# Distances of two graphs side by side in TensorE's row places

## The chip, the core and the metric

The kernel runs on one core of one Trainium2 chip. The metric is the time of one execution on the device, in microseconds. A core has a matrix engine (TensorE, "PE" in the profile, its weight loads "PEld"), a vector engine (VectorE, "DVE"), a scalar engine (ScalarE, "ACT"), a general engine (GpSimd, "POOL") and a queue engine (SyncE, "SP") which here only issues transfers. TensorE writes its products into PSUM, of which the pools of a stage take eight banks; the tiles in SBUF have 128 rows (partitions). Everything is in 32-bit floats.

## What is computed

64 graphs of 256 nodes with 256 features go through two layers. Layer 0 multiplies the normalised adjacency with the normalised rows and then with a weight. Layer 1 has a 17-tap convolution along the nodes, a message step, and a gated update. Cut to what matters here:

```python
# layer 0, h = relu(layernorm(x))
x = x + relu(einsum('bnm,bmf->bnf', norm_adj, h) @ W.T + b)
# layer 1, h = relu(layernorm(x))
x_conv = relu(bn2(conv17(relu(bn1(conv1(h))))) + h)
s    = h @ w_se.T + b_se                      # three numbers per node
dist = |s_n|^2 + |s_m|^2 - 2 s_n . s_m        # 256 x 256 per graph
A    = exp(-dist)                             # times the mask, here adj
x_nmp = einsum('bnm,bmd->bnd', A, relu(h @ w_msg.T + b_msg))
x = x + gru(concat(x_conv, x_nmp), h)
```

The distance matrix is what the change is about. It is written as a product with five rows: three hold the coordinates s, one holds ones against minus half the squared length, one the reverse. exp(2 x product) is then exp(-dist).

## The kernel before

**Stage one** (the loop over n, `for n in range(B + 4)`) takes the graphs through layer 0 and the front of layer 1 in a software pipeline. In turn n, TensorE gets, in this order: `turn_h` of graph n-2 (transposes, tile ht), `aggregate` of n (ag), `turn_cols` of n-3 (st), `turn_adj` of n+1 (at), `pass_messages` of n-4 (nm), `messages` of n-2 (ms), `distance` of n-3 (di), `project` of n (o) and `conv1` of n-2 (c). Between them calls of `item` slip in one piece of the convolution: first filter products (fs, `filter_part`), then spectra (df, `spectrum`), then products with the transformed filter (y, `product`). How many pieces enter is set by `pace`: its first entry is added at every call, its second is the running sum, and a piece goes when the sum passes one. While the filter is made only two of the eight calls per turn count.

The order on each engine is the order in which the program writes the instructions: `Pinned` keeps it on TensorE, ScalarE, VectorE and GpSimd. `after(k, f)` puts f off to the (k+1)-th following `beat`, so that the reading of a product is written some products later. `beat(us)` also releases the waiting elementwise work of the inverse transform (`Paced`), a share of the given time per engine. The transfers on SP are placed by a scheduler, as early as their tiles are free, but are then issued strictly in that order.

**The distance of one graph.** `messages` leaves three extra columns per node. `columns` (VectorE) copies them into the constant tile `cols` four times, at columns 0, 32, 64 and 96, and adds the squared lengths. `turn_cols` transposes `cols` (128 nodes x 128 columns, two blocks of nodes). ScalarE copies rows 0 to 36 into L and rows 64 to 100 into R. `distance` makes two products, one for each half of the nodes, with five rows each, at rows 0 and 32, into two banks: two row places of TensorE. ScalarE then takes two exponentials (tile e), GpSimd multiplies with the transposed adjacency `adjT` (tile aT), and a turn later `pass_messages` uses aT with the messages (msg).

The PSUM pool `ps` of stage one has five banks in rotation: ht, ag, st, at, nm, di, o, fs, df and y all take theirs from it. ms and c have banks of their own, which ScalarE fills with the bias ahead of the products.

**Filter.** When the tap weights are transposed and written out (wtd), two tiles tp are loaded from them by ten transfers, `pace[:] = FILTER / 2, -5.0` is set, and 32 filter pieces follow. Each has four products of 17 rows and 512 columns at rows 0, 32, 64 and 96 into four banks. The rest of the tp loads is issued as the pieces go.

**Convolution.** Its filter parts wf (71 per group of 16 graphs, 256 KB each) are loaded into `WF` buffers, and each product's end releases the next load. The inverse transform ends with `residual_load`, which brings rows of h2 into `hr` buffers.

**Gate stages.** Four times: the outputs are transposed (`turn_outputs`, yt), the spectra and first three products of the next group follow, then 16 graphs of gates, each with up to six products: one between the gates, the rest in a burst. Before the first, four products named `first_` with a 128-row identity touch the four gate banks.

Of the kernel before, what the change touches and what calls it, by code (L numbers as in the profile page):

```python
# [11 lines left out]
FP = mybir.dt.float32  # L12
AF = mybir.ActivationFunctionType
# [172 lines left out]
def gnn_kernel(  # L186
# [11 lines left out]
    P = 128  # L198
# [48 lines left out]
    def after(beats, go):  # L247
        due.append([beats, go])
# [66 lines left out]


    PARTS = [(0, 0), (0, 1)] + [(u, k) for u in range(1, UNITS) for k in (2, 1, 0)]
    WF = 8

    def wf_load(n):  # L320
        if n < len(PARTS):
# [43 lines left out]
    def inverse_after(u):  # L365

        if u == 7:
            inverse_three()
            for n in NS[:4]:
                residual_load(n)  # L370
        if u >= 8 and u % 4 == 3:
            inverse_group(u // 4 - 2)
        if u == UNITS - 1:
            inverse_last()
# [52 lines left out]
    def residual_load(n):  # L427

        src = h2_d[cv.q].rearrange("(p i) d -> p i d", i=OUT)
        cv.hr[n] = hr = cv.stream.tile([P, 2, D], FP, tag="hr", name=f"hr_{cv.q}_{n}", bufs=4)  # L430
        nc.sync.dma_start(hr, src[:, n::16, :])

    def inverse_last():
# [79 lines left out]
        for i in range(4):  # L513
            outs = points(i)
            paced.do(1, lambda i=i: done.add(i))
            paced.barrier(4, lambda i=i: i in done)
            for z in outs:
                outputs(NS[k], z, hold[k % 2])
                if k + 4 < len(NS):
                    paced.do(4, lambda k=k: residual_load(NS[k + 4]))  # L520
                residual(k + 2)
                k += 1

# [21 lines left out]
    with ExitStack() as one:  # L545
# [15 lines left out]
        def bank(name):  # L561
            return ps.tile([P, 512], FP, tag="ps", name=name)
# [20 lines left out]

        cols = wts.tile([P, NB, P], FP, tag="cols", name="cols")
        nc.gpsimd.memset(cols, 0.0)
        for c0 in (3, 35, 68, 100):
            nc.gpsimd.memset(cols[:, :, c0 : c0 + 1], 1.0)

        prep_stack = ExitStack()
        prep = prep_stack.enter_context(tc.tile_pool(name="prep", bufs=1))
# [425 lines left out]
        def conv1(g):  # L1018
            t = to_rows(g, "c1", w1T)

            def keep():
                h1 = work.tile([P, NB, D], FP, tag="c1", name=f"c1o_{g}")
                act.activation(h1, t, AF.Relu)
                nc.sync.dma_start(h1_d[g].rearrange("p (c d) -> p c d", c=NB), h1)
            after(1, keep)
            if g + 1 < B:
                after(2, lambda: own_bank("c1", g + 1, b1B))

        def messages(g):

            s, t = st[g], to_rows(g, "ms", wmT)

            def columns():
                four = cols.rearrange("p b (k w) -> p b k w", w=32)
                vec.tensor_copy(
                    four[:, :, :, 0:3],
                    t[:, :, D : D + 3].unsqueeze(2).broadcast_to([P, NB, 4, 3]),
                )
                sq = small.tile([P, NB, 3], FP, tag="sq", name=f"sq_{g}")
                vec.scalar_tensor_tensor(  # L1040
                    sq, cols[:, :, 0:3], -0.5, cols[:, :, 0:3], ALU.mult, ALU.mult
                )
                twice = sq.unsqueeze(2).broadcast_to([P, NB, 2, 3])
                vec.tensor_reduce(four[:, :, 0:2, 4], twice, AX.X, ALU.add)
                vec.tensor_reduce(four[:, :, 2:4, 3], twice, AX.X, ALU.add)

            def keep():
                s["msg"] = work.tile([P, NB, D], FP, tag="ms", name=f"mso_{g}", bufs=3)
                act.activation(s["msg"], t[:, :, :D], AF.Relu)
            after(1, columns)  # L1050
            after(1, keep)
            if g + 1 < B:
                after(2, lambda: own_bank("ms", g + 1, bmB))

        def turn_cols(g):
            s = st[g]
            t = bank(f"st_{g}")
            for nb in range(NB):
                pe.transpose(t[:, nb * P : (nb + 1) * P], cols[:, nb, :], ident)

            def keep():
                for key, p0 in (("L", 0), ("R", 64)):
                    s[key] = work.tile([37, N], FP, tag=key, name=f"{key}_{g}", bufs=1)
                    act.copy(s[key], t[p0 : p0 + 37, :N])
            after(1, keep)

        def distance(g):
            s = st[g]
            ts = [bank(f"di_{g}_{mc}") for mc in range(NB)]
# [7 lines left out]
            def weigh():  # L1077
                s["e"] = work.tile([P, NB, N], FP, tag="e", name=f"e_{g}")
                for mc in range(NB):
                    act.activation(s["e"][:, mc, :], ts[mc][:, :N], AF.Exp, scale=2.0)  # L1080

            def mask():
                s["aT"] = work.tile([P, NB, N], FP, tag="aT", name=f"aT_{g}")
# [91 lines left out]

        FILTER, SPECTRA, PRODUCTS = 2, 5, 3
        filtering = []
        for n in range(B + 4):
            even, odd = n % G == 0, n % G == 1
            if filtering and not items:  # L1180
                filtering.clear()
# [62 lines left out]
            if n >= 2 and later:  # L1244
                for go in later.pop(0):
                    go()
                if not later:
                    while due:
                        beat(0.0)
                    prep_stack.close()  # L1250
                    spec_stack = ExitStack()
                    spec = spec_stack.enter_context(tc.tile_pool(name="spec", bufs=1))
                    tab = spec.tile([P, 3 * UNITS], FP, tag="tab", name="tab")
                    nc.sync.dma_start(tab, nc.inline_tensor(filter_table(), name="tab_c").ap())
                    tp = {k: filter_load(k) for k in range(2)}
# [250 lines left out]
    for q in range(1, GROUPS + 1):  # L1506
# [7 lines left out]
        todo = []  # L1514
        if q < GROUPS:
            conv_begin(q)
            for k in range(WF):
                wf_load(k)
            for g in range(NG):
                for cb in range(DC):  # L1520
                    spectrum(g, cb)
            for u in range(1, AHEAD):
                sums(u)
            todo = [lambda u=u: product(u) for u in range(UNITS)]
            for _ in range(LEAD):
                todo.pop(0)()
# [45 lines left out]
```

## Time and profile before

| | us |
|---|---|
| median of 3 runs | 2120.74 |
| lowest, highest | 2119.82, 2123.37 |
| the profiled execution | 2119.19 |
| its span on the core | 2116.7 |
| TensorE busy in the span | 2068.2 |
| VectorE, ScalarE, GpSimd busy | 1414.1, 1017.0, 1098.9 |
| stage one, start to the first yt | 889.0 |
| spent on di by TensorE (256 records) | 44.8 |

How to read the rows. A 32-bit product is two records of TensorE, so one graph's distance, two products, is a group of four. Durations overlap, because products are pipelined: the cost of a group is the distance from its start to the next group's start. A timeline row gives start, duration, engine, line, operation, what is written from what, the number of instructions, and in brackets the idle time before it with what ended it. All work goes through one recording helper, so nearly every row has line 102: rows are told apart by tiles. The granted clock is the share of full speed that TensorE was given.

### The profile page before, as it was taken

What the parts mean: (1) busy time and instruction counts of PE and PEld (TensorE: products, weight loads), DVE (VectorE), ACT (ScalarE), POOL (GpSimd) and SP (SyncE); (2) the same over time, 40 slices, a digit from 0 to 9 for tenths busy, and PEclk for the clock granted to TensorE, in tenths of its full rate; (3) what the DMA queues carried; (4) which work ended last, traced back from release to release, by engine and by line L of the source; (5) the groups of instructions that cost most, each with busy time, mean ns of one, the idle gap of its engine ahead of it and who ended that gap; (6) DMA issues with size and microseconds to landing.
All of it is one profiled execution on the core that took longest, in us unless ns stands there. A gap on an engine that the chain in (4) does not pass through costs nothing. (4 is left out here: it accounts for less than half of the span.)

```text
span 2116.7 us, 31285 instructions
## 1 busy us (share of the span) xinstructions
PE 2068.2 (98%) x9977; PEld 1737.2 (82%) x9977; DVE 1414.1 (67%) x3207; ACT 1017.0 (48%) x2203; POOL 1098.9 (52%) x1309
## 2 busy tenths in 40 slices
PE   8979999999999999999999999999999999999998
PEld 6866666888888887688888888888888888888887
DVE  6545656545578998615989923989933889974444
ACT  5856666665455676542334442234452234443333
POOL 4333323334675565327766626767635767744343
PEclk9989999999999999999999999999999999999999
DMA  8696777755766554456533356533345523423331
GB/s 300 227 236 216 223 224 235 260 178 177 241 209 205 190 181 156 168 176 207 169 105 120 119 167 202 184 94 121 120 145 180 188 85 110 125 82 93 90 100 60
DMA packets 292458, 352.86 MB, mean 167 GB/s; under 512 B 19491, under 2 KB 232118, under 8 KB 291638
## 3 DMA queue, kind: packets, MB, share of 16 engines
q1 hardware_dynamic: 291680, 346.26, 52.2%
q0 software_dynamic: 288, 4.46, 0.6%
q8 instruction: 80, 1.31, 0.3%
q14 instruction: 84, 0.69, 0.1%
q10 hardware_dynamic: 326, 0.14, 0.0%
HBM read 224.43 MB, written 126.35 MB: 166 GB/s over the span
## 5 line engine op out<-in xcount | busy, mean ns | idle before, releaser
L102 DVE TENSOR_TENSOR Xf<-y,k 128x256 f32<-128x256 f32 x184 | 69.0, 416 | 180.9 <-PE y L102 178.6
L102 DVE SCALAR_TENSOR_TENSOR Xf<-Xf 128x256 f32<-128x256 f32 (+1 forms) x248 | 184.0, 757 | 6.5 <-ACT Xf L102 5.4
L102 PE MATMUL ta<-T,S 128*128 128x256 f32 x768 | 186.6, 379 | 0.0
L102 PE MATMUL y<-wf,Xf 128*128 128x256 f32 x768 | 182.5, 380 | 1.7 <-DVE Xf L102 1.4
L102 POOL TENSOR_TENSOR aT<-e,adjT 128x512 f32<-128x512 f32 x64 | 82.3, 1286 | 189.3 <-ACT e L102 189.3
L102 POOL TENSOR_TENSOR rz<-u,p 128x256 f32<-128x256 f32 x64 | 47.7, 745 | 244.8 <-ACT u L102 244.8
L102 ACT ACTIVATE rz<-rz 128x512 f32<-128x512 f32 x128 | 80.3, 627 | 180.3 <-DVE rz L102 180.3
L102 PEld LDWEIGHTS y<-wf,Xf 128*128 128x128 f32 x768 | 144.4, 190 | 24.4 <-DVE Xf L102 2.6
L102 PEld LDWEIGHTS ta<-T,S 128*128 128x128 f32 x768 | 145.9, 190 | 19.8
L102 PE MATMUL n<-wiT,hx 128*128 128x256 f32 x512 | 152.3, 379 | 0.0
L102 DVE SCALAR_TENSOR_TENSOR h2l<-rz,h2l 128x256 f32<-128x256 f32 x128 | 102.8, 803 | 53.4 <-POOL h2l L102 53.4
L102 POOL TENSOR_TENSOR xs<-Xf 128x256 f32<-128x256 f32 x92 | 71.0, 777 | 126.0 <-ACT Xf L102 64.1
L102 POOL TENSOR_TENSOR rs<-ve,mhalf 128x2 f32<-128x2 f32 (+1 forms) x65 | 46.9, 722 | 169.7 <-DVE nm L102 165.4
L102 POOL TENSOR_TENSOR adjH<-adjT,eye 128x512 f32<-128x512 f32 x64 | 82.0, 1282 | 97.4 <-ACT adjT L102 97.1
L102 PE MATMUL n<-whT,hx 128*128 128x256 f32 x512 | 131.4, 379 | 0.0
L102 PE MATMUL n<-wiT,xcT 128*128 128x256 f32 x512 | 131.4, 379 | 0.0
L102 PE MATMUL o<-w0T,aggT 128*128 128x256 f32 x512 | 127.8, 392 | 3.1 <-ACT aggT L102 3.1
L102 PE MATMUL ag<-adjH,hs 128*128 128x256 f32 x512 | 123.5, 384 | 4.7 <-POOL adjH L102 3.3
L102 PE MATMUL nm<-aT,mso 128*128 128x256 f32 x512 | 123.2, 384 | 4.2 <-POOL aT L102 3.4
L102 PE MATMUL ms<-wmT,h2T 128*128 128x259 f32 x512 | 124.7, 385 | 2.7 <-DVE h2T L102 2.7
L102 PE MATMUL c<-w1T,h2T 128*128 128x256 f32 x512 | 125.8, 390 | 0.0
L102 DVE BATCH_NORM_STATS2 st<-x 128x6 f32<-128x256 f32 x256 | 103.4, 404 | 28.2 <-DMA x<-in_x_dram 28.2
(185 smaller groups left out, 5319.7 us busy)
## 6 DMA issues: line engine op xcount, KB each, us to landing
wf<-wfd SPq DMA_DIRECT2D x284, 256.0 KB
wfd<-fo SPq DMA_DIRECT2D x32, 576.0 KB
x2d<-x SPq DMA_DIRECT2D x64, 256.0 KB
h2d<-h SPq DMA_DIRECT2D x64, 256.0 KB
hTd<-h2T SPq DMA_DIRECT2D x64, 256.0 KB
h1d<-c1o SPq DMA_DIRECT2D x64, 256.0 KB
xnd<-xnT SPq DMA_DIRECT2D x64, 256.0 KB
h1l<-h1d SPq DMA_DIRECT2D x64, 256.0 KB
```

The source lines that it names most:

```text
L102: return self.tc.keep_in_program_order(getattr(self.engine, op)(*args, **kwargs))
```

## The change

- `cols` gets a second side and each graph of a pair its own columns. Sides L and R are separate 128-column halves; row place 32k holds half m of the nodes of graph b, with k = 2m + b. `columns` of a graph writes its own places, `turn_cols` and `distance` run in even turns only and serve two graphs. There are four transposes per pair, one copy each for L and R with all 128 rows, and four products at four row places into four banks.
- The exponentials of the second graph are put one beat behind those of the first, its mask two beats behind.
- `turn_cols` and `distance` are at n-4, `pass_messages` at n-5, the loop has one turn more; adjT gets a sixth buffer, msg a fourth. The last `conv1` moves from turn B+1 to B+2.
- The filter's pace starts at -7 in place of -5.
- WF is 6 in place of 8, the residual loads have 3 buffers in place of 4 and are asked for three outputs ahead. In the gate stages the first wf loads are written between the last spectra, no longer ahead of all.
- The `first_` products use 32 rows each, at four row places.

```diff
-    WF = 8
+    WF = 6
...
-            for n in NS[:4]:
+            for n in NS[:3]:
                 residual_load(n)
...
-        cv.hr[n] = hr = cv.stream.tile([P, 2, D], FP, tag="hr", name=f"hr_{cv.q}_{n}", bufs=4)
+        cv.hr[n] = hr = cv.stream.tile([P, 2, D], FP, tag="hr", name=f"hr_{cv.q}_{n}", bufs=3)
...
-                if k + 4 < len(NS):
-                    paced.do(4, lambda k=k: residual_load(NS[k + 4]))
+                if k + 3 < len(NS):
+                    paced.do(4, lambda k=k: residual_load(NS[k + 3]))
...
-        cols = wts.tile([P, NB, P], FP, tag="cols", name="cols")
+        cols = wts.tile([P, NB, 2, P], FP, tag="cols", name="cols")
         nc.gpsimd.memset(cols, 0.0)
-        for c0 in (3, 35, 68, 100):
-            nc.gpsimd.memset(cols[:, :, c0 : c0 + 1], 1.0)
+        for k in range(4):
+            nc.gpsimd.memset(cols[:, :, 0, 32 * k + 3 : 32 * k + 4], 1.0)
+            nc.gpsimd.memset(cols[:, :, 1, 32 * k + 4 : 32 * k + 5], 1.0)
...
-                s["adjT"] = work.tile([P, NB, N], FP, tag="adjT", name=f"adjT_{g}", bufs=5)
+                s["adjT"] = work.tile([P, NB, N], FP, tag="adjT", name=f"adjT_{g}", bufs=6)
...
-                four = cols.rearrange("p b (k w) -> p b k w", w=32)
+                own = cols.rearrange("p b s (m k w) -> p b (s m) k w", m=2, k=2)[:, :, :, g % 2]
                 vec.tensor_copy(
-                    four[:, :, :, 0:3],
+                    own[:, :, :, 0:3],
                     t[:, :, D : D + 3].unsqueeze(2).broadcast_to([P, NB, 4, 3]),
                 )
...
-                s["msg"] = work.tile([P, NB, D], FP, tag="ms", name=f"mso_{g}", bufs=3)
+                s["msg"] = work.tile([P, NB, D], FP, tag="ms", name=f"mso_{g}", bufs=4)
...
         def turn_cols(g):
             s = st[g]
-            t = bank(f"st_{g}")
-            for nb in range(NB):
-                pe.transpose(t[:, nb * P : (nb + 1) * P], cols[:, nb, :], ident)
+            t = bank(f"st_{g}").rearrange("p (s n) -> p s n", s=2)
+            for side in range(2):
+                for nb in range(NB):
+                    pe.transpose(
+                        t[:, side, nb * P : (nb + 1) * P],
+                        cols[:, nb, side, :], ident,
+                    )
 
             def keep():
-                for key, p0 in (("L", 0), ("R", 64)):
-                    s[key] = work.tile([37, N], FP, tag=key, name=f"{key}_{g}", bufs=1)
-                    act.copy(s[key], t[p0 : p0 + 37, :N])
+                for side, key in enumerate("LR"):
+                    s[key] = work.tile([P, N], FP, tag=key, name=f"{key}_{g}", bufs=1)
+                    act.copy(s[key], t[:, side])
             after(1, keep)
 
         def distance(g):
-            s = st[g]
-            ts = [bank(f"di_{g}_{mc}") for mc in range(NB)]
-            for mc in range(NB):
-                own_rows = slice(32 * mc, 32 * mc + 5)
+            both = [(b, mc) for mc in range(NB) for b in range(2)]
+            ts = [bank(f"di_{g + b}_{mc}") for b, mc in both]
+            for k, (b, mc) in enumerate(both):
+                own_rows = slice(32 * k, 32 * k + 5)
                 pe.matmul(
-                    ts[mc][:, :N], s["L"][own_rows, mc * P : (mc + 1) * P],
-                    s["R"][own_rows, :], start=True, stop=True,
+                    ts[k][:, :N], st[g]["L"][own_rows, mc * P : (mc + 1) * P],
+                    st[g]["R"][own_rows, :], start=True, stop=True,
                 )
...
-            after(1, weigh)
-            after(2, mask)
+            after(1, lambda: weigh(0))
+            after(2, lambda: weigh(1))
+            after(2, lambda: mask(0))
+            after(4, lambda: mask(1))
...
-        for n in range(B + 4):
+        for n in range(B + 5):
...
-            if 3 <= n <= B + 2:
-                turn_cols(n - 3)
+            if even and 4 <= n <= B + 2:
+                turn_cols(n - 4)
...
-            if n >= 4:
-                pass_messages(n - 4)
+            if n >= 5:
+                pass_messages(n - 5)
...
-            if 3 <= n <= B + 2:
-                distance(n - 3)
+            if even and 4 <= n <= B + 2:
+                distance(n - 4)
...
-            if 2 <= n <= B + 1:
+            if 2 <= n <= B:
                 conv1(n - 2)
+            elif n == B + 2:
+                conv1(B - 1)
...
-                    pace[:] = FILTER / 2, -5.0
+                    pace[:] = FILTER / 2, -7.0
...
-    for tag, bufs in (("ta", 1), ("tc", 1), ("n", 2)):
-        for k in range(bufs):
-            t = ps_gate.tile([P, 2 * D], FP, tag=tag, name=f"first_{tag}_{k}", bufs=bufs)
-            pe.matmul(t, ident, brzB, start=True, stop=True)
+    for r, tag in enumerate(("ta", "tc", "n", "n")):
+        t = ps_gate.tile([P, 2 * D], FP, tag=tag, name=f"first_{r}", bufs=1 + (tag == "n"))
+        at = slice(32 * r, 32 * (r + 1))
+        pe.matmul(t, ident[at, :], brzB[at, :], start=True, stop=True)
...
             conv_begin(q)
-            for k in range(WF):
-                wf_load(k)
             for g in range(NG):
+                if g >= NG - WF:
+                    wf_load(g - NG + WF)
                 for cb in range(DC):
                     spectrum(g, cb)
```

More of the change, by code (lines that the diff above doesn't have):

```diff
@@ L1033, in columns @@
             def columns():
-                four = cols.rearrange("p b (k w) -> p b k w", w=32)
+                own = cols.rearrange("p b s (m k w) -> p b (s m) k w", m=2, k=2)[:, :, :, g % 2]
                 vec.tensor_copy(
-                    four[:, :, :, 0:3],
+                    own[:, :, :, 0:3],
                     t[:, :, D : D + 3].unsqueeze(2).broadcast_to([P, NB, 4, 3]),
                 )
+                s3 = own[:, :, 0, 0:3]
                 sq = small.tile([P, NB, 3], FP, tag="sq", name=f"sq_{g}")
-                vec.scalar_tensor_tensor(
-                    sq, cols[:, :, 0:3], -0.5, cols[:, :, 0:3], ALU.mult, ALU.mult
-                )
+                vec.scalar_tensor_tensor(sq, s3, -0.5, s3, ALU.mult, ALU.mult)
                 twice = sq.unsqueeze(2).broadcast_to([P, NB, 2, 3])
-                vec.tensor_reduce(four[:, :, 0:2, 4], twice, AX.X, ALU.add)
-                vec.tensor_reduce(four[:, :, 2:4, 3], twice, AX.X, ALU.add)
+                vec.tensor_reduce(own[:, :, 0:2, 4], twice, AX.X, ALU.add)
+                vec.tensor_reduce(own[:, :, 2:4, 3], twice, AX.X, ALU.add)
             def keep():
-                s["msg"] = work.tile([P, NB, D], FP, tag="ms", name=f"mso_{g}", bufs=3)
+                s["msg"] = work.tile([P, NB, D], FP, tag="ms", name=f"mso_{g}", bufs=4)
                 act.activation(s["msg"], t[:, :, :D], AF.Relu)
@@ L1077, in weigh @@
-            def weigh():
-                s["e"] = work.tile([P, NB, N], FP, tag="e", name=f"e_{g}")
+                    ts[k][:, :N], st[g]["L"][own_rows, mc * P : (mc + 1) * P],
+                    st[g]["R"][own_rows, :], start=True, stop=True,
+                )
+            def weigh(b):
+                s = st[g + b]
+                s["e"] = work.tile([P, NB, N], FP, tag="e", name=f"e_{g + b}")
                 for mc in range(NB):
-                    act.activation(s["e"][:, mc, :], ts[mc][:, :N], AF.Exp, scale=2.0)
@@ L1082, in mask @@
-            def mask():
-                s["aT"] = work.tile([P, NB, N], FP, tag="aT", name=f"aT_{g}")
+                    act.activation(s["e"][:, mc, :], ts[2 * mc + b][:, :N], AF.Exp, scale=2.0)
+            def mask(b):
+                s = st[g + b]
+                s["aT"] = work.tile([P, NB, N], FP, tag="aT", name=f"aT_{g + b}")
                 pool.tensor_tensor(s["aT"], s["e"], s["adjT"], ALU.mult)
-            after(1, weigh)
-            after(2, mask)
+            after(1, lambda: weigh(0))
```

## The prediction

> **What bounds the kernel now.** I read the page's busy rows first, then where TensorE waits, then the stretches around those waits. TensorE is the bound nearly everywhere: busy for 2068.2 of 2116.7 us, and the work that this change touches is TensorE's own.
>
> ```profile
> PE 2068.2 (98%) x9977; PEld 1737.2 (82%) x9977; DVE 1414.1 (67%) x3207; ACT 1017.0 (48%) x2203; POOL 1098.9 (52%) x1309
> ```
>
> So first: what does one distance cost TensorE? The timeline of TensorE in a steady stretch of stage one (start, duration, group):
>
> ```profile
> 709.59 1.91 PE L102 MATMUL ms<-wmT,h2T 128*128 128x259 f32 x8
> 711.43 0.70 PE L102 MATMUL di<-R,L 5*128 5x256 f32 x4
> 712.06 1.99 PE L102 MATMUL o<-w0T,aggT 128*128 128x256 f32 x8
> 713.89 1.89 PE L102 MATMUL c<-w1T,h2T 128*128 128x256 f32 x8
> 715.62 0.60 PE L102 MATMUL ht<-ident,h 128*128 128x128 f32 x4
> ```
>
> Read starts, not durations. From di to o is 0.63. From ms to di is 1.84, and eight ms matmuls take 1.75 where no di follows: 0.09 more. From o to c is 1.83, against 1.73 from c to ht, also eight matmuls of 256 columns: 0.10 more. One distance costs 0.63 + 0.09 + 0.10 = 0.83 us, for two products side by side.
>
> Four row places side by side exist already, in the filter's products (fs). Same view, two of its groups:
>
> ```profile
> 165.66 1.68 PE L102 MATMUL fs<-tp,tab 17*72 17x512 f32 x8
> 167.27 2.02 PE L102 MATMUL ms<-wmT,h2T 128*128 128x259 f32 x8
> ...
> 171.77 1.09 PE L102 MATMUL fs<-tp,tab 17*72 17x512 f32 x8
> 172.79 1.99 PE L102 MATMUL c<-w1T,h2T 128*128 128x256 f32 x8
> ```
>
> With all banks free four products of 512 columns take 1.02 (171.77 to 172.79), about the length of one. At 165.66 the same group takes 1.61: its fourth bank was still held.
>
> Two places where TensorE is not the bound matter here. At 144 us it waits 11.47 us, and the chain of waits leads to a load (TensorE, ScalarE and VectorE timelines):
>
> ```profile
> 155.42 2.25 PE L102 MATMUL fs<-tp,tab 17*72 17x512 f32 x4 [11.47 <-ACT e L102]
> 157.60 3.58 PE L102 MATMUL c<-w1T,h2T 128*128 128x256 f32 x8
> ```
> ```profile
> 153.83 0.60 ACT L102 ACTIVATE mso<-ms 128x512 f32<-128x512 f32 x1 [13.73 <-DVE cols L102]
> ```
> ```profile
> 151.49 0.43 DVE L102 BATCH_NORM_STATS2 st<-x 128x6 f32<-128x256 f32 x1 [15.13 <-DMA x<-in_x_dram]
> ```
>
> VectorE is stuck on the row moments of x_14, ScalarE on VectorE, TensorE on both. The c after it takes 3.58 instead of 1.89: the granted clock averages 0.68 between 140 and 160 us. The second place is the end of stage one:
>
> ```profile
> 874.86 0.70 PE L102 MATMUL di<-R,L 5*128 5x256 f32 x4
> 878.59 3.78 PE L102 MATMUL nm<-aT,mso 128*128 128x256 f32 x8 [3.03 <-POOL aT L102]
> 883.09 2.08 PE L102 MATMUL first_ta<-brzB,ident 128*128 128x512 f32 x2 [0.72 <-ACT xnT L102]
> 884.95 1.91 PE L102 MATMUL first_tc<-brzB,ident 128*128 128x512 f32 x2
> 886.66 2.49 PE L102 MATMUL first_n<-brzB,ident 128*128 128x512 f32 x4
> 888.99 0.27 PE L102 MATMUL yt<-ident,Xf 128*128 128x128 f32 x1
> ```
>
> **The change, part by part.**
>
> *Distances.* 64 visits become 32. A visit's surroundings stay (0.09 + 0.10); its middle is 0.63 plus two more starts, 7 ns apart in the fs group: 0.65. So 32 x (2 x 0.83 - 0.84) = 26.1 us less. The transposes of cols are as many as before (two per graph, 0.11 each). The copies of L and R halve (64 x 0.36 of ScalarE less), and VectorE's four small operations per graph stay.
>
> *What the four banks may cost.* Stage one has five rotating banks; a pair now holds four. The Trainium skill (TensorEngine Tiling (Array Packing), Performance Considerations, PSUM Bottleneck) says that tiling speeds up TensorE but not the emptying of PSUM, which may become the bound. In the rows at 129 to 132 us the exponentials start 1.55 us after di starts (131.29 against 129.74, behind mso and a bias copy) and two take 0.65. Four end at 2.85, with some 0.2 to reach TensorE 3.05. By the rule TensorE would stand there from 2.46 (0.63 + o's 1.83) on: 0.6 x 32 = 19 us given back in place of the 4.4 below, and a time of 2104.5. By the rows it mostly does not: o takes the fifth bank, and behind it c1 has its own. Only the filter's second group follows o directly with rotating banks; there 8 to 9 pairs wait about 0.5, +4.4. Against it stands the filter's first group: in odd graphs no L and R copies precede adjT, so its fourth bank is free sooner, 8 x 0.6, and in even ones the doubled transposes give the copies 0.2 more, -1.6. I take -2; bounds -7 and +4.4.
>
> *Messages a graph later.* n + 5 in place of n + 4; the extra turn holds one product that was there before, so it is a shift. adjT and msg get a buffer each. The first mask ends some 3.5 us after di starts (1.29 of GpSimd behind the exponentials), its nm comes after o, c, ht, ag and at, at 6.8; the second is needed a graph later. I cost it at nothing; if that cover were gone, 1.3 per pair.
>
> *The stall at 144 us.* Filter -5 to -7 moves the first filter product by two slots, one graph. x_14 stays behind the ten tp loads on SP, and its moments stay ahead of cols_9 on VectorE, so the stall stays. Only how early it begins changes: TensorE has less to do ahead of it (nm_7, the first fs group, di_8 left for later: 1.73 + 1.5 + 0.43, some 3.9 with st). The release is the second half of hs_12 on ScalarE, about 4.3 us after x_14's first moments, and the load comes earlier by what TensorE gained until graph 7. That is at most 4.2 (0.83 x 5 - 0.84 x 2 + one nm), and about 2.8 where ScalarE, without idle time from 56 to 67 us, holds the pace. The next ag starts at 151.5 - 2.8 + 4.3 = 153.0; adding 3.9 of owed work and 2.8 for the halved clock, equal progress stands at 159.7 against 161.45: 1.75 gained where the distances counted so far (9 visits against 4.5 pairs) claim 3.7. So +2; bounds -2 and +4.
>
> *End of stage one.* Before, from ms_63's end (869.94) to yt (888.99): 19.05. After, from the same point: wait for cols_63 1.3, st 0.44, nm_61 1.73 (earlier work before), switch 0.1, di pair 0.64, switch 0.1, c1_63 1.73 (moved here), wait for aT_62 about 0.6, nm_62 and nm_63 3.46, xnT's bank 1.0, four first products side by side 1.15. Sum 12.25, less nm_61 10.5, so 8.5 shorter, of which 0.83 is already a distance: -7.7. The clock stays up[...]. VectorE's and GpSimd's inverse work is now issued later; its first outputs end at about +8, before yt at +12.25. If it is late: down to -4; if the waits vanish: -9.
>
> *Less time per graph under VectorE.* From 700 to 870 us VectorE is busy 147.4 of 170 us and TensorE already loses about 4 us in waits for h2T, hs and pre. TensorE's share per graph falls by 0.41, VectorE's does not. +2.5; bounds 0 and +6.
>
> *WF 8 to 6, residual buffers 4 to 3.* I matched the queue's packets in order with SP's issues: in the bursts of five products a wf lands 1.6 to 3.4 us after its issue, and with eight buffers the tightest has 3.0 us in hand. Two fewer take away 2 x 0.865: 1.27 left. Residual loads land 2.3 us after issue; moved one output later they still come 0.7 us ahead of GpSimd. In the changed program the gate stages' first six wf loads still stand on SP behind the last products, ahead of the stage. All at nothing; bounds -1 and +3.
>
> *Start.* The zeroing of cols is twice as wide and ahead of eye on GpSimd: +0.3.
>
> Sum: -26.1 - 2 + 2 - 7.7 + 2.5 + 0.3 = -31.0. The profiled execution took 2119.19 (span 2116.7), so 2088.2; the median of the runs, 2120.74, lies 1.55 above it: **2089.7 us**.
>
> **Rivals.**
>
> *Slower: TensorE waits once per pair for the second graph's exponentials or mask.* The second exponentials and mask are issued a beat and two beats behind the first. For it: ScalarE carries four at once, as in the rule above. Against it: 3.3 us lie between the first mask and its nm, a graph more for the second, and o has the fifth bank. It decides from 31.0/32 = 0.97 us per pair on; at 1.3, the whole second mask uncovered, the time is 2131. Chance 0.05.
>
> *Half the gain: VectorE or the banks give it back.* Both at their bad ends (+3.5, +6.4) and the end of stage one at -4: 2103; the rule's sum, 2104.5, belongs here. Chance 0.15.
>
> *More: the stall at 144 us goes.* If x_14 comes before TensorE needs VectorE, 11.5 of waiting and 3.7 of slow clock go, and the +2: about 2073. Against it: the ten tp loads keep their place ahead of x_14. Chance 0.07.
>
> *The four do not run side by side.* Then a visit takes 1.28 and only the switches are saved, 0.19 x 32 = 6: 2110. Against it: fs at 171.77. Chance 0.04.
>
> **How the numbers follow.** The likeliest case holds 0.69, its own range 2081 to 2099. Reaching into the half-gain case above and partly toward the vanished stall below gives 2079 to 2104. About 0.2%, 4 us, is what a measurement can tell from no change. Only the slow case ends above 2125, so slower 0.05; within, 0.02 from the edges of the second and fourth; faster 0.93.
>
> **What would show it.** Right: di in 32 groups of eight, 0.64 to 0.65 each; a stall of 10 us or more on x_14 still there, now at ag; yt 8 us nearer to ms_63; the granted clock near 1 at the end of stage one; wf never in TensorE's waits. Wrong: di groups split by bank waits, TensorE waiting for e or aT in most pairs, wf among its waits in the bursts of five products, or VectorE above nine tenths with waits of a microsecond per graph.

## The result and the profile after

| | us |
|---|---|
| before, median of the runs beside it | 2120.51 |
| after, median (lowest, highest) | 2087.19 (2086.44, 2090.9) |
| ratio after to before, 95% interval | 0.9844 (0.9827 to 0.9861) |
| the profiled execution after, its span | 2086.44, 2084.7 |

The forecast of 2089.7 was 2.5 us too high. That closeness is luck: four of its terms are off by 2 to 6 us each, and they cancel. Where the time went, stretch by stretch, in the two traces (idle is TensorE's idle time in the stretch, gaps of all sizes summed):

| stretch | before | after |
|---|---|---|
| start to the stall on x_14: idle | 10.8 | 12.5 |
| the stall | 11.5 | 10.2 |
| stall to 680 us: idle | 2.0 | 0.7 |
| 680 us to the last ms: idle | 4.2 | 8.9 |
| start of the last ms | 868.1 | 836.8 |
| last ms to the first yt (idle) | 20.8 (3.9) | 15.9 (4.2) |
| first yt to the first df behind it (idle) | 7.8 (0.0) | 11.6 (2.4) |
| from there to the end | 1219.9 | 1220.4 |

The page of the kernel after, TensorE's row:

```profile
PE 2029.4 (97%) x9977; PEld 1728.8 (83%) x9977; DVE 1413.3 (68%) x3207; ACT 987.4 (47%) x2139; POOL 1101.0 (53%) x1313
```

TensorE is busy 38.8 us less with the same number of records, and its idle time has grown: 97% in place of 98%. A steady pair of the kernel after, in TensorE's timeline (start, duration, group):

```profile
697.58 1.91 PE L102 MATMUL ms<-wmT,h2T 128*128 128x259 f32 x8
699.42 0.71 PE L102 MATMUL di<-R,L 5*128 5x256 f32 x8
700.07 1.99 PE L102 MATMUL o<-w0T,aggT 128*128 128x256 f32 x8
701.90 1.89 PE L102 MATMUL c<-w1T,h2T 128*128 128x256 f32 x8
703.62 0.60 PE L102 MATMUL ht<-ident,h 128*128 128x128 f32 x4
```

Four products take 0.65 from di to o where two took 0.63. Of the 32 visits 31 are groups of eight records, 0.644 in the median; the one at 604 us is cut into six and two by a wait of 0.27. The turn of an odd graph has no di, and there ms costs 1.75 and o 1.73, so the switches on both sides (0.09 and 0.10) are saved too. 32 x (2 x 0.826 - 0.839) = 26.0.

The filter's groups, same view (behind nm and behind o in an odd turn, then behind nm in an even one):

```profile
169.28 1.44 PE L102 MATMUL fs<-tp,tab 17*72 17x512 f32 x8
170.65 2.02 PE L102 MATMUL ms<-wmT,h2T 128*128 128x259 f32 x8
172.51 1.89 PE L102 MATMUL o<-w0T,aggT 128*128 128x256 f32 x8
174.32 1.09 PE L102 MATMUL fs<-tp,tab 17*72 17x512 f32 x8
...
207.95 1.22 PE L102 MATMUL fs<-tp,tab 17*72 17x512 f32 x8
209.10 1.58 PE L102 MATMUL ms<-wmT,h2T 128*128 128x259 f32 x6
```

From start to start they take, behind nm, 1.37 in odd and 1.15 in even turns (before 1.61 or 1.92), behind o 1.24 or 1.02. Leaving out the first one of each trace, 31 groups take 37.0 us after and 46.9 before. In the kernel before, two of them took 3.07, which the prediction had not looked for. One of the two, TensorE's timeline before:

```profile
297.32 1.08 PE L102 MATMUL fs<-tp,tab 17*72 17x512 f32 x4
299.38 1.08 PE L102 MATMUL fs<-tp,tab 17*72 17x512 f32 x4 [0.98 <-DVE pre L102]
300.39 3.43 PE L102 MATMUL c<-w1T,h2T 128*128 128x256 f32 x8
303.62 0.89 PE L102 MATMUL ht<-ident,h 128*128 128x128 f32 x4
```

Its third product waits for VectorE to finish reading o's bank, and here c and ht behind it run at half speed: 3.23 and 0.73 from start to start, where 1.83 and 0.44 are usual.

The stall on x_14 is still there, now at ag. VectorE's and TensorE's timelines after:

```profile
146.45 0.43 DVE L102 BATCH_NORM_STATS2 st<-x 128x6 f32<-128x256 f32 x1 [13.62 <-DMA x<-in_x_dram]
```
```profile
139.82 0.60 PE L102 MATMUL ag<-adjH,hs 128*128 128x256 f32 x2
150.60 2.93 PE L102 MATMUL ag<-adjH,hs 128*128 128x256 f32 x6 [10.18 <-ACT hs L102]
```

Between 680 us and the last ms TensorE waits for VectorE's copy h2T. The longest of these waits cost more than itself:

```profile
777.17 3.53 PE L102 MATMUL ms<-wmT,h2T 128*128 128x259 f32 x8 [2.07 <-DVE h2T L102]
780.49 2.11 PE L102 MATMUL o<-w0T,aggT 128*128 128x256 f32 x8
```

From start to start ms and o take 3.32 and 1.94 here, where 1.75 and 1.73 are usual: 1.8 of half-speed clock, which is no idle time and so is not in the table.

The end of stage one after, in the timelines of TensorE, of ScalarE and of SP's issues:

```profile
844.72 3.72 PE L102 MATMUL nm<-aT,mso 128*128 128x256 f32 x16 [0.28 <-POOL aT L102]
851.55 1.14 PE L102 MATMUL first<-brzB,ident 32*128 32x512 f32 x8 [3.12 <-ACT xnT L102]
852.63 0.48 PE L102 MATMUL yt<-ident,Xf 128*128 128x128 f32 x1
852.89 0.42 PE L102 MATMUL yt<-ident,scr 128*128 128x128 f32 x1
...
857.88 1.94 PE L102 MATMUL yt<-ident,Xf 128*128 128x128 f32 x14 [2.44 <-ACT xcT L102]
```
```profile
850.94 0.56 ACT L102 COPY xnT<-nm 128x512 f32<-128x512 f32 x1
...
857.14 1.26 ACT L102 ACTIVATE xcT<-yt,sh 128x512 f32<-128x512 f32 x2 [2.71 <-DMA xnd<-xnT]
```
```profile
853.04 0.53 SPq L431 DMA_DIRECT2D hr<-h2d  x1
853.68 0.54 SPq L1113 DMA_DIRECT2D xnd<-xnT  x1
```

The first yt comes 36.4 us earlier than before (852.6, was 889.0), but df only 32.6: yt now stops for 2.44 us. ScalarE may not write xcT until the last xnT has been stored, whose memory xcT takes over, and that store is issued on SP behind a residual load.

### The profile page after: what moved, and what is told of

Read it like the earlier page. It is cut to its first block, busy times and chain, and to the rows that moved or that the text cites. A ratio compares the mean times of both kernels' runs of the same rounds, so it can differ in the third digit from the quotient of the medians.

```text
span 2084.7 us, 31178 instructions
## 1 busy us (share of the span) xinstructions
PE 2029.4 (97%) x9977; PEld 1728.8 (83%) x9977; DVE 1413.3 (68%) x3207; ACT 987.4 (47%) x2139; POOL 1101.0 (53%) x1313
## 5 line engine op out<-in xcount | busy, mean ns | idle before, releaser
L102 POOL TENSOR_TENSOR rs<-ve,mhalf 128x2 f32<-128x2 f32 (+1 forms) x65 | 46.9, 722 | 231.5 <-DVE nm L102 226.6
L102 PE MATMUL ag<-adjH,hs 128*128 128x256 f32 x512 | 123.4, 384 | 15.9 <-ACT hs L102 10.8
L102 PEld LDWEIGHTS ms<-wmT,h2T 128*128 128x128 f32 x512 | 95.9, 191 | 34.9 <-issue 13.5
```

The lines of the kernel that those rows point to most:

```text
L102: return self.tc.keep_in_program_order(getattr(self.engine, op)(*args, **kwargs))
```

## The experiments

Times are medians, each with its ratio to the kernel before on the same chip; the kernel before had 2120.3 to 2122.2 there.

**1. Pairs split.** The second graph's two products in the odd turn, all else as changed.

```diff
...
-            if even and 4 <= n <= B + 2:
-                distance(n - 4)
+            if 4 <= n <= B + 3:
+                distance(n - 4 - n % 2, n % 2)
```

> The changed kernel (2087.2), but the second graph of a pair has its two distance products in the following, odd turn: 64 visits of two products again, at the same row places, with the transposes, the copies of L and R, the extra buffers, the end of stage one and the filter's start all left as changed. If each saved visit is worth what the prediction counted, 2 x 0.83 - 0.84 per pair comes back: +26.1, 2113. Rival from the trace after: the time per graph between 700 and 850 us is already set by VectorE there, so that 12 to 16 pairs lost half of their saving; then what comes back is 18 to 21, 2105 to 2108. Second reading: the filter's first groups take 1.26 on average where they took 1.7, and two long groups of 3.07 are gone; if that comes from the distance's banks being absent in odd turns, it comes back too, 7 to 11 us, and the first rival is hidden under it; if it comes from the halved copies and the filter's new place, the groups stay at 1.26.

Measured: 2105.8, ratio 0.9933 (0.9921 to 0.9945), so the split costs 18.6 us and not 26.1. TensorE's timeline with the pairs split, an odd turn and the last nm:

```profile
196.48 1.11 PE L102 MATMUL fs<-tp,tab 17*72 17x512 f32 x8
197.52 2.02 PE L102 MATMUL ms<-wmT,h2T 128*128 128x259 f32 x8
199.47 0.70 PE L102 MATMUL di<-R,L 5*128 5x256 f32 x4
200.10 1.99 PE L102 MATMUL o<-w0T,aggT 128*128 128x256 f32 x8
...
864.66 1.99 PE L102 MATMUL nm<-aT,mso 128*128 128x256 f32 x8 [3.02 <-POOL aT L102]
```

The visit costs the old 0.63 and the switches, 26.0 in all, so something comes back the other way. Pairs do cost banks: with them, 31 filter groups take 37.0 and not 35.5, and two di behind y wait 0.5 and 1.0. The stall is 1.2 shorter without pairs, and between 680 us and the last ms TensorE waits 5.0 in place of 8.9. Together 1.5 + 1.5 + 1.2 + 3.9 = 8.1, and half clock behind the stall and at 777 us takes 2.5 more from the pairs. Against that, the split kernel loses 4.8 between its last ms and df that are no distances: its last nm stands 3.02 for aT, yt 4.21. In the two traces 26.0 - 8.1 - 2.5 + 4.8 = 20.2, where the spans differ by 19.5. So the 18.6 hold a worse end of stage one, and the pairs by themselves bring less. The filter's groups behind nm stay short (1.04 and 1.46). So the shorter groups behind nm do not come from pairing.

**2. The filter's start back at -5.**

```diff
-                    pace[:] = FILTER / 2, -7.0
+                    pace[:] = FILTER / 2, -5.0
```

> The changed kernel with the filter's start back at -5. The prediction's step: the stall on x_14 stays either way, and -7 only moves work that is done ahead of it or after it, so within 2 us of 2087.2. Theory from the trace after: the inverse work of the first group now ends too late for the end of stage one (TensorE waits 3.1 us ahead of first and 2.4 us in yt, both behind ScalarE's and VectorE's inverse work); with the filter one graph earlier that work ends a graph earlier and 3 to 5 us go: 2082 to 2084. Rival: the filter's place in the turns is what took the long groups of 3.07 away; then they come back and the time is 2088 to 2091.

Measured: 2085.55, ratio 0.9836 (0.9823 to 0.985), 1.6 below the changed kernel, with intervals that overlap. The theory of a late inverse transform got less than it asked: the wait ahead of first fell from 3.12 to 0.72, but yt's rose from 2.44 to 3.34. The rival fell too: no long group came back.

**3. Second tile of taps behind x_14.**

```diff
-                    tp = {k: filter_load(k) for k in range(2)}
+                    tp = {0: filter_load(0)}
+                    after(19, lambda: tp.update({1: filter_load(1)}))
```

> The changed kernel with the second tile tp (five of the ten loads of taps) loaded some two turns later, behind the load of x_14 and not ahead of it. Theory of the prediction: x_14 is late because it stands behind ten tp loads in the queue and in transfer; with half of them gone it lands some 7 us earlier, and of the wait of 10.18 us and the 2.8 us of halved clock at least 8 go: 2076 to 2079. Rival: x_14 is late because its buffer comes free late (x2d_9 is stored at 131.2) and the transfers share the same engines; then 3 us or less go, 2084 or more, and the first filter group of the second tile waits for its taps.

Measured: 2075.62, ratio 0.9793 (0.978 to 0.9807), 11.6 less. VectorE's and TensorE's timelines of this kernel:

```profile
134.42 0.43 DVE L102 BATCH_NORM_STATS2 st<-x 128x6 f32<-128x256 f32 x1 [2.26 <-DMA x<-in_x_dram]
```
```profile
139.15 1.89 PE L102 MATMUL ag<-adjH,hs 128*128 128x256 f32 x8
140.88 0.60 PE L102 MATMUL st<-ident,cols 128*128 128x128 f32 x4
...
147.89 1.31 PE L102 MATMUL fs<-tp,tab 17*72 17x512 f32 x8
```

VectorE waits 2.26 for x_14 and not 13.62, and the ag that was cut in two is whole again, 1.73 from start to start. The whole stall and its slow clock are gone. So x_14 was late because of the five tp loads moved here, and the change leaves all ten ahead of it. SP's issue of x_14 in the changed kernel, then in this one:

```profile
135.74 0.39 SPq L825 DMA_DIRECT2D x<-in_x_dram  x1
```
```profile
127.22 0.39 SPq L825 DMA_DIRECT2D x<-in_x_dram  x1
```

It is issued 8.5 earlier, and the first moments follow 7.2 behind the issue where it was 10.7: the place on SP is the larger part, the transfer itself the rest. The rival of the vanished stall had put this at 2073.

**4. The last store of xnT on ScalarE's queue.**

```diff
-                nc.sync.dma_start(xn_d[g].rearrange("p (c n) -> p c n", c=DC), xn)
+                e = act if g == B - 1 else nc.sync
+                e.dma_start(xn_d[g].rearrange("p (c n) -> p c n", c=DC), xn)
```

> The changed kernel with one transfer moved: the store of xnT of the last graph is issued from ScalarE's own queue, not from SP's. Theory: in the trace after, yt waits 2.44 us for ScalarE, which waits for the end of that store (xcT takes its place in memory), and the store was issued at 853.68 on SP, behind a residual load that waits for one of only three hr buffers, though xnT was written by 851.5. Without the residual load ahead of it the store lands 2 us earlier: 2085.2, and the wait in yt drops below 0.5. Rival (the prediction's own: three hr buffers cost nothing): the store is limited by other work, the time is the same to 0.5 us.

Measured: 2086.63, ratio 0.9846 (0.9832 to 0.9859): the same time as the change. TensorE's timeline of this kernel:

```profile
856.79 2.06 PE L102 MATMUL yt<-ident,Xf 128*128 128x128 f32 x14 [0.27 <-ACT xcT L102]
...
863.29 5.13 PE L102 MATMUL df<-dft,h1l 128*128 128x240 f32 x24
870.38 5.98 PE L102 MATMUL df<-dft,h1l 128*128 128x240 f32 x20 [1.96 <-DMA h1l<-h1d]
```

The mechanism was right, the wait in yt is gone (2.44 to 0.27). The gain was not: df now waits 1.96 for the next h1l, 0.78 in the changed kernel.

**5. The first products over all 128 rows again.**

```diff
-        at = slice(32 * r, 32 * (r + 1))
-        pe.matmul(t, ident[at, :], brzB[at, :], start=True, stop=True)
+        pe.matmul(t, ident, brzB, start=True, stop=True)
```

> The changed kernel with the four products named first again over all 128 rows, one after the other. The prediction counted 4.1 - 1.15 = 2.95 us for them at the end of stage one, so 2090.1. Theory from the trace after: yt stops after its first dozen anyway, at 857.9, for a store of xnT that has nothing to do with the first products; with them 3 us longer the dozen ends at 857.4 and the stop shrinks from 2.4 us to nothing. Then the time is the same to 0.7 us, 2087 to 2088.

Measured: 2087.45, ratio 0.9837 (0.9824 to 0.9851): the same. TensorE's timeline:

```profile
850.52 5.40 PE L102 MATMUL first<-brzB,ident 128*128 128x512 f32 x8 [3.12 <-ACT xnT L102]
855.75 0.27 PE L102 MATMUL yt<-ident,Xf 128*128 128x128 f32 x1
...
856.63 2.53 PE L102 MATMUL yt<-ident,Xf 128*128 128x128 f32 x18
```

The four products take 5.23 in place of 1.08 and yt then has no wait at all. They fill the time in which yt would wait: the store of xnT decides when xcT can be written, whatever TensorE does ahead of it.

**6. The kernel before with the new buffers alone.** WF 6, three residual buffers asked for three outputs ahead, wf loads between the last spectra.

```diff
-    WF = 8
+    WF = 6
...
-                if k + 4 < len(NS):
+                if k + 3 < len(NS):
```

> The kernel before with the buffers of the change alone: six wf buffers for eight, three residual buffers for four with the loads asked for three outputs ahead, and the first wf loads of a gate stage written between the last spectra. The prediction: nothing, within 1 us of 2120.5, and wf in no wait of TensorE. Rival: the residual loads, which now stand on SP until one of three buffers is free, hold up the store of the last xnT behind them, and yt gets a wait of 1 to 3 us: 2121.5 to 2123.5.

Measured: 2122.73 beside 2121.76, ratio 1.0002 (0.9994 to 1.001). Nothing, as predicted. In the kernel before, three residual loads already stand on SP ahead of the last store of xnT, from 877.47 on. The store was issued at 884.02 and yt starts at 888.99, so there is room for them. One thing does change in the trace, TensorE's waits over the whole span:

```profile
PE y L102 <- DMA wf<-wfd: 1.0, 3, 0.6
```

The kernel before and experiment 9, with eight wf buffers, have no such wait.

**7. h2T copied by ScalarE from graph 48.**

```diff
-                vec.tensor_copy(s["hT"], t)
+                (act.copy if g >= 48 else vec.tensor_copy)(s["hT"], t)
```

> The changed kernel with one VectorE operation per graph moved: from graph 48 on ScalarE copies h2T out of PSUM (some 0.6 us each, 16 of them). Theory: VectorE sets the pace from 680 us to the end of stage one, its inverse work comes ahead of h2T's copy, and 5.9 of the 8.86 us in which TensorE waits there are for h2T. With h2T from ScalarE (busy 94 of 150 us there) most of these waits go: 4 to 5 us less, 2082 to 2083. Rival: the waits only change their name, because the same inverse work then holds up pre, x or cols on VectorE or hs and aggT on ScalarE: less than 1.5 us gained, 2085.7 or more.

Measured: 2084.07 (2080.9 to 2085.2), ratio 0.9813 (0.98 to 0.9827), 3.1 less by the medians. TensorE's waits (total, times, longest) between 680 and 850 us in the changed kernel, then in this one:

```profile
PE ms L102 <- DVE h2T L102: 5.9, 5, 2.1
PE o L102 <- ACT xnT L102: 0.9, 1, 0.9
PE st L102 <- DVE cols L102: 0.8, 1, 0.8
...
```
```profile
PE first L102 <- ACT xnT L102: 3.1, 1, 3.1
PE nm L102 <- POOL aT L102: 1.9, 2, 1.6
PE ag L102 <- ACT hs L102: 1.0, 3, 0.5
PE ag L102 <- POOL adjH L102: 1.0, 1, 1.0
```

h2T has left the list, and the idle time from 680 us to the last ms falls from 8.9 to 4.6. Some of it comes back as aT and hs; the 3.1 ahead of first lies behind 850 us in the changed kernel and stands in both.

**8. Both: tp behind x_14, start at -5.**

```diff
-                    tp = {k: filter_load(k) for k in range(2)}
+                    tp = {0: filter_load(0)}
+                    after(19, lambda: tp.update({1: filter_load(1)}))
...
-                    pace[:] = FILTER / 2, -7.0
+                    pace[:] = FILTER / 2, -5.0
```

> The second tile tp loaded behind x_14 and the filter's start at -5, both. Alone they gave 2075.6 and 2085.6 where the change gave 2087.2. If they do different things (one takes the stall at 144 us, the other brings the inverse work of the first group a graph forward), the gains add: -11.6 - 1.6, 2074. Rival: with -5 the first filter product comes before its taps have landed or so close behind x_14 that a part of the stall comes back: 2076 to 2080. Without a stall the start at -5 puts filter products ahead of the point where they stood in the kernel before, so their long groups could come back as well.

Measured: 2075.76, ratio 0.9779 (0.9766 to 0.9792), the time of experiment 3. The 1.6 of experiment 2 did not add. No long group and no stall came back.

**9. The kernel before with -7 alone.**

```diff
-                    pace[:] = FILTER / 2, -5.0
+                    pace[:] = FILTER / 2, -7.0
```

> The kernel before with the filter's start at -7, that part alone. In the changed kernel the 31 filter groups behind the first take 37.0 us, in the kernel before 46.9; with the distances split again they stay at 35.6 and with -5 at 37.2. Two differences are left that could have shortened them: the copies of L and R, which both kernels with short groups make in even turns only, or a new place in the turns together with something else. If the copies do it, the groups here stay at 45 to 48 and the time at 2119 to 2122, the stall on x_14 above 10 us. Rival (place): groups below 40 and 2110 to 2114.

Measured: 2112.14, ratio 0.9962 (0.9948 to 0.9975), 8.1 less. Both readings on record were half right. The groups behind nm stay long (28.3 us for 16, against 20.0 in experiment 1), so the place is not what shortens those; that leaves the halved copies of L and R, which no run changes alone. But both groups of 3.07 are gone, with the slow c behind one of them, and so the place shortens these. The stall is 9.16 in place of 11.47. The end of stage one, by windows: length, then busy time and records of each engine, the granted clock, DMA share, GB/s. First before, then with -7:

```profile
866.00:890.00 24.00, 19.84 (x68) 12.76 (x69) 13.30 (x22) 10.74 (x27) 9.13 (x9) 0.79 0.40 130
```
```profile
860.00:884.00 24.00, 18.79 (x91) 13.04 (x90) 16.39 (x27) 12.61 (x31) 9.06 (x8) 1.00 0.33 110
```

The last nm, which waited 3.03 for aT and then ran 3.78 at half clock, waits 2.21 here and runs at full clock:

```profile
873.12 1.99 PE L102 MATMUL nm<-aT,mso 128*128 128x256 f32 x8 [2.21 <-POOL aT L102]
```

**10. The late store and late gate weights.** As experiment 4, with whT and wiT (2.4 MB) loaded from ScalarE's queue behind the third graph's spectra.

```diff
-    nc.sync.dma_start(whT, wh_d)
-    nc.sync.dma_start(wiT, wi_d)
...
+                if q == 1 and g == 3:
+                    act.dma_start(whT, wh_d)
+                    act.dma_start(wiT, wi_d)
+                    gate_weights()
```

> The changed kernel with the last xnT's store on ScalarE's queue, as in the run before on this, and the gate weights whT and wiT (some 2.2 MB) loaded later, from ScalarE's queue behind the third graph's spectra, not from SP at the end of stage one. With the store alone yt lost its wait, 2.44 to 0.27, but 1.96 us came back where df waits for the fourth h1l, which is loaded behind whT, wiT and hx. Theory: the end of stage one is bound by those transfers; with the weights out of the way the df wait falls below 0.5 and the gain of 2 us shows at the first product: 2084 to 2085. Rival: hx alone or the store's own transfer keeps h1l late, or the weights now come late for the first gates: 2086.5 or more.

Measured: 2087.98, ratio 0.9849 (0.9836 to 0.9863). The wait moved once more, from df's fourth h1l to a later one, in TensorE's timeline:

```profile
869.74 1.86 PE L102 MATMUL df<-dft,h1l 128*128 128x240 f32 x8 [0.24 <-DMA h1l<-h1d]
875.11 5.16 PE L102 MATMUL df<-dft,h1l 128*128 128x240 f32 x16 [3.51 <-DMA h1l<-h1d]
```

The theory was right that the weights' transfer delays h1l, and wrong that there was a better moment three graphs later.

**11 and 12. The sums.** First 3, 7 and 10 together, then 3 and 7 alone, which is:

```diff
-                vec.tensor_copy(s["hT"], t)
+                (act.copy if g >= 48 else vec.tensor_copy)(s["hT"], t)
...
-                    tp = {k: filter_load(k) for k in range(2)}
+                    tp = {0: filter_load(0)}
+                    after(19, lambda: tp.update({1: filter_load(1)}))
```

> All that shortened the changed kernel or should: the second tile tp behind x_14 (-11.6 alone), h2T copied by ScalarE from graph 48 (-3.1 alone), and the late store and late gate weights of the run before this (-2 expected). If the three places are separate the gains add: 2070.5 to 2072.5. Rival: the tail, where TensorE waits 3.1 us ahead of first for ScalarE's inverse work, takes back what h2T gains, as it took part of it before (5.9 us of waits gone, 3.1 gained): 2073 to 2075.

> The changed kernel with the second tile tp behind x_14 and h2T copied by ScalarE from graph 48, without the moved store and without the late gate weights. Alone they gave -11.6 and -3.1: 2072.5 if they add. The run with the store and the weights moved as well gave 2071.8, and its trace shows the wait in yt gone but 4.3 us of waiting ahead of the first product, 0.9 in the changed kernel: so the two moved transfers should have brought nothing, and this run equals that one within 1 us. Rival: they brought 1.5 us or more here, and this run is at 2073.3 or above.

Measured: 2071.78, ratio 0.977 (0.9757 to 0.9783), and 2071.9, ratio 0.9764 (0.975 to 0.9777). The gains of 3 and 7 add (2072.5 by the parts), and the moved store and weights bring nothing. The kernel with 3 and 7 beats both kernels: 15.3 us below the changed one, by three lines.

## Why the prediction came out right, step by step

*Distances, -26.1: right.* 26.0 from the steady rows. That the four run side by side, which the rival of 2110 denied, is shown by 0.644 for eight records. Undoing it costs 18.6 (experiment 1): the step gave the cost on TensorE, and the rest is what the pairs take elsewhere, below, less what the split loses at its own end of stage one.

*Four banks, -2: the largest miss, a mis-sized term.* Filter groups -9.9, waits of di behind y +1.5: -8.4, beyond the bound of -7. Of its three parts, the filter's second group cost +0.2 in every second one (+1.3 over 15), not +0.5 (+4.4). The first group gained 27.3 - 20.1 = 7.2 over 16 of them where 6.4 was predicted. The halved copies of L and R stay the likely reason (experiment 1 keeps the gain without pairs, experiment 9 has none of it), but the split by turn came out the other way round. The step gave odd turns 0.6 and even ones 0.2, and that is how it is with the pairs split (1.04 in odd, 1.46 in even turns). In the changed kernel odd turns take 1.37 and even ones 1.15: in the odd turn shown, ScalarE's h waits 0.23 for GpSimd's nmr at 168.03, the copy adjT behind it ends at 169.59, and the last weights of fs are loaded at 169.64. The third was not in the working at all: two groups of 3.07, 4.1 us. In them the third product was handed o's bank, which VectorE was still reading; they disappear with -7 alone, with pairs alone, and with both. *The rule weighed there*, that emptying PSUM becomes the bound, would have given back 19 us. The wait it describes exists, but 0.2 at a time in every second filter group behind o, and in the two visits behind y; from 160 to 680 us TensorE's waits for e and k come to 0.8 us in all. By the rule's 2104.5 the answer would have been 17 us off.

*Messages a graph later, 0: right.* No nm waits for aT between 160 and 680 us. Behind 680 us two do, 0.8 in all, where before it was 3.4.

*The stall, +2: wrong in sign.* The stall stayed at ag as said, but x_14's first moments came at 146.45, 5.0 earlier, where the step allowed 2.8 for ScalarE's pace and 4.2 at most. By graph 7's ms TensorE had gained 3.5 (113.83, was 117.31); SP issued the load 4.5 earlier (135.74, was 140.22), and from issue to moments it took 0.6 less. What brought the load forward by more than TensorE's gain is open. The wait is 1.3 shorter. In the kernel before, -7 alone gains 2.3 there and leaves 8.1 in all; in the paired kernel it gains nothing against -5 (2087.2 and 2085.6). So this edit has no price of its own: the long groups and the half-speed last nm, which it takes away in the kernel before, are gone with the pairs anyway.

*End of stage one, -7.7: wrong.* From the last ms to the first yt 5.0 were saved, with a nm of 1.7 more inside, and 0.8 of it counted as a distance, so 5.9 by the prediction's count; then 3.8 were lost in yt, 2.1 net. The step that failed is "its first outputs end at about +8, before yt": it asked when yt's inputs are ready and not when its output may be written. The store behind the last xnT decides that (experiments 4 and 5), so the 2.95 for the first products were worth nothing. Two other terms failed as well: xnT's bank took 3.1 and not 1.0, since ScalarE's copy stands behind inverse work; and with that the clock did not stay up, the rows of yt behind it run 0.42 for 0.27.

*VectorE, +2.5: right in kind, too small.* The idle time grew by 4.7 (4.2 to 8.9), and with the 1.8 of half clock behind the wait at 777 us it is 6.5, past the bound of 6. Experiment 7 shows the cause by taking it away.

*WF and residual buffers, 0: right in the time, not in the wait.* Experiment 6 shows no cost, and in the profiled execution of the changed kernel TensorE waits nowhere for wf. But with six buffers it does in eight of the twelve traces on record, 0.5 to 2.0 us in all, most in experiment 12. So the margin of 1.27 that the step found is at times used up; the cost stays inside the bound of +3. The residual load ahead of the last store cost 2.2 in yt, which would have been lost in df all the same (experiment 4). Nothing shows that the three buffers put it there: with four of them residual loads stand ahead of that store as well, and in experiment 9 yt then waits 1.59.

*Start, +0.3: not resolved.* Idle time ahead of the stall was 1.7 more, but lies between 10.8 and 13.2 in runs whose programs do not differ there.

Summed: -26.0 - 8.4 - 1.3 + 1.7 + 4.7 - 2.1 and +0.5 behind are -30.9. The slow c and ht at 300 us, gone as well, are another -1.7, and the half clock at 777 us is +1.8: -30.8 of the -32.1 by which the spans differ, with 1.3 not placed. Of the rivals, the slower one had nothing for it: no nm waits for a mask between 160 and 680 us, and behind that only 0.8 in all. "Half the gain" did not come, though two of its three bad ends did (VectorE's, with the half clock counted, and the end of stage one's; both went past it), because the filter's groups paid for them.

What stays open is why those two groups, and not the others, met o's bank unread, and how the 8.1 of -7 alone divide: the two groups account for 4.1 and the 1.7 behind one of them, less 1.0 for more groups of 1.92, the stall for 2.3 of idle time, and the starts of the two traces differ as well.

## What to carry to other kernels

When a stage is made shorter, ask of its first output not only when its inputs are ready but when its memory is free, and by which transfer: here the last store of the stage before. And before pricing a phase constant such as the filter's start, try it in both kernels: it was worth 8.1 us in one and nothing in the other, where the long groups and the half-speed nm that it takes away were gone already. A long stall in the profile that a change leaves alone is worth an experiment of its own; two lines at the loads of taps were worth a third of the whole change.

## What the hardware showed

In these traces, from 60 us on, half clock came with or just behind every wait of TensorE of 3.03 us or more: 3.03 before and 3.12 after at the end of stage one, and the 10 us of the stall. Waits of 2.21 (experiment 9) and 3.02 (experiment 1) left the nm behind them at full speed, 1.99. So in the last nm 0.8 us of waiting more, 3.03 for 2.21, went with another 1.8. The Trainium skill (TensorE: Matmul & The Clock Gate, Why this matters for your kernels) puts the limit at about 3 us of idle time. That agrees with these rows, but a shorter wait is not safe: ms at 777.17 after ran at half clock behind a wait of 2.07 (the granted clock is 0.50 from 777.5 to 780.9), and in experiment 3 the same ms at 763.25 ran at full speed behind 2.08 (1.00 from 763.3 to 767). In the same way c at 300.39 before ran at half clock behind a wait of 0.98, and the same wait at 242.56 was followed by a c of full speed. What decides below 3 us, no run here shows.
